# Probability blocks from SBUF to SBUF by sixteen small transfers a unit, in place of a way through DRAM

## The chip, the cores and the metric

The kernel runs on one core of one Trainium2 chip. The metric is the device time of one launch in microseconds (us); lower is better. A second clock is the profile: one execution recorded by the hardware profiler, whose span goes from the first to the last instruction. Engines are named PE (TensorE), PEld (its weight loads), DVE (VectorE), ACT (ScalarE), POOL (GpSimd) and SP (SyncE, which in this kernel does nothing but issue transfers).

## The reference

`x` has 8 batches of 256 tokens of 512 features, all in float32. It is normalised, goes through causal attention with 32 query heads and 8 key heads of 128 features, and the result is gated by the SiLU of a routed low-rank expert layer and added to `x`. The part that matters here is the middle of the attention:

```python
q = (xn @ wq.T) ; k = (xn @ wk.T) ; v = (xn @ wv.T)      # 32, 8 and 8 heads of 128
q, k = rope(q), rope(k)                                  # four query heads share a key head
scores = einsum('bhqd,bhkd->bhqk', q, k) / sqrt(128) * scale + causal
probs = softmax(scores)
attn = einsum('bhqk,bhkd->bhqd', probs, v)
out = x + (attn @ wo.T) * silu(ffn(xn))
```

## The kernel before

**Tiling.** The work goes in four rounds `tb` of two batches. In a round there are eight steps `g`, one for each key head, and in a step two *units*, one for each batch: 64 units in all. A unit is the attention of four query heads over 256 tokens. `softmax` (line 748) holds its first half and `values` (line 873) its second. PE also makes queries, keys and values by a Strassen-like scheme of seven products (`quad`, line 553), and the output projection by the same scheme (`out_project`, line 908).

**Softmax of a unit.** PE makes the scores with, in each of the 128 rows, one of 32 queries of one of four heads (row = 32 x head + query). DVE subtracts the maximum, ACT takes exponentials into the one tile `probs_sb` (`p` in the profile), DVE divides by the row totals. The values product needs the probabilities with the *keys* in the rows. DVE transposes 32x32 blocks, in two instructions, into the tile `blocks` (line 811), of which there is one for the whole kernel. That leaves each block inside its own group of 32 rows: group h of `blocks` holds, for head h, the four key groups j side by side. What is still missing is a move between groups: block (h, j) must go from rows 32h.. to rows 32j.., into the tile `pT`, of which there are three.

**The way through DRAM.** `spread` (line 822) writes `blocks` to a DRAM tile `there` in four transfers, one for each head, of 192 KB each. `gather` (line 832) reads it back into `pT` in one transfer of 768 KB. All five are issued on SP. SP waits for the second DVE transpose before the four, and for the landing of all four before the fifth.

**Values of a unit.** `values` makes two PE pieces, k = 0 for heads 0 and 1 and k = 1 for heads 2 and 3, of six matrix products each (`av`). Both wait for the unit's gather.

**The order of the work.** [...]That order comes from a planner (`Plan`, line 170) that simulates the kernel when it is built. Each job has an engine, an assumed time `takes`, and a `lag` after it until its result is there (a transfer's landing); `HOP`, 0.18 us, is added between jobs. PE's jobs are laid in a preferred sequence; every other job has a due time. A job can open a `hold` (take a buffer) and close it (give it back); `rooms` (line 298) has one room for `p`, one for `blocks` and three for `pT`. An engine takes the ready job with the earliest due time that has room. `softmax` adds `out_` (SP, 2.4 us, lag 3.4) and `in_` (SP, 0.35 us, lag 7.0); the hold on `blocks` ends with `out_`. The tile framework then puts in the semaphore waits. SP's transfers use eight semaphores in rotation, so the ninth transfer waits until the first has landed.

**Other work on SP.** Loads of `x`, of the gates and of the input for the last sum, the stores, and in three rounds the moves of the next round's normalised input (`norm`, lines 379 and 390): eight transfers of 128 KB to DRAM (`turned`) and eight back (`XB`). Weights are loaded by POOL's queue.

In the profile every instruction has line 118, that of a helper that issues them all, so the rows are told apart by tile names.

Of the kernel before, what the change touches and what calls it, by code (L numbers as in the profile page):

```python
# [37 lines left out]
F32 = mybir.dt.float32  # L38
# [6 lines left out]
P = 128  # L45
B, S, D = 8, 256, 512
H, KV, HD = 32, 8, 128
G = H // KV
# [7 lines left out]
NTB = B // NB  # L56
NT = TB // P
DC = D // P
BLK = 32
NI = S // BLK  # L60
NQ = P // BLK
# [108 lines left out]
class Plan:  # L170
# [10 lines left out]
    def add(self, engine, takes, what, after=(), opens=(), closes=(), near=None, lag=0.0):  # L181
        after = [a for a in after if a]
        job = Job(engine, takes, what, after, opens, closes, near, lag, len(self.jobs))
        for a in after:
            a.then.append(job)
        for hold in closes:
            hold.readers += 1
        self.jobs.append(job)
        return job
# [67 lines left out]
def layer(ctx: ExitStack, tc: tile.TileContext, x, wquad, woquad, raT, bT, table, out):  # L257
    nc = InOrder(tc)
# [4 lines left out]
    three = pool("three", 3)  # L263
# [28 lines left out]
    add = plan.add  # L292
    rooms = {}

    def hold(tag):
        return Hold(rooms[tag])
# [7 lines left out]
    keys, vals, queries, probs, attn, acc = {}, {}, {}, {}, {}, {}  # L304
# [443 lines left out]
    def softmax(tb, g, b):  # L748

        n = f"{tb}_{g}_{b}"  # L750
        box = {}
        p = probs_sb
# [12 lines left out]
        def scores(rows):  # L765
            kk = kbox["k"][:, g % G].rearrange("p i s -> p (i s)")
            sc = box["sc", rows] = ps_sc.tile(
                [P, width(rows)], F32, tag="sc", name=f"sc{n}_{rows[0]}"
            )
            for i, size, cols in spans(rows):  # L770
                first = P if i >= NQ else 0
                nc.tensor.matmul(
                    sc[:, cols], lhsT=qbox["q"][:, i].rearrange("p h s -> p (h s)"),
                    rhs=kk[:, first : first + size], start=True, stop=True,
                )
# [35 lines left out]
        def transpose(late):  # L811


            if not late:
                box["blocks"] = one.tile([P, NQ, 3 * P], F32, tag="blocks", name=f"blocks{n}")
            to, of = (
                (box["blocks"][:, :, 2 * P :], p[:, NQ:, NQ:]) if late
                else (box["blocks"][:, :, : 2 * P], p[:, :NQ])
            )
            nc.vector.transpose(to, of.rearrange("p j i c -> p j (i c)"))  # L820
# [11 lines left out]
        def gather():  # L832
# [3 lines left out]
                in_=box["there"].rearrange("j a h c -> (j a) (h c)"),  # L836
            )

        takes = lambda rows: sum(max(0.235, (i + 1) * 0.054) for i in rows)
        pieces, exps = [], []  # L840
        ph, bh, th = hold("p"), hold("blocks"), hold("pT")
        for rows in groups:
            sh, zh = hold("sc"), hold("z")
            sc = add(
                "pe", takes(rows), lambda r=rows: scores(r), after=[q_done, k_done], opens=[sh],
                closes=[qh, kh],
            )
# [7 lines left out]
                    opens=[ph] if rows == groups[0] else [], near=(sc, 2.5))  # L855
            )
            pieces.append(sc)
        sc = pieces[-1]
# [4 lines left out]
            near=(sc, 4.0),  # L863
        )
        t1 = add(
            "dve", 0.6, lambda: transpose(True), after=[t0], closes=[ph], near=(sc, 4.5)
        )
        out_ = add("sp", 2.4, spread, after=[t1], closes=[bh], near=(sc, 5.0), lag=3.4)
        in_ = add("sp", 0.35, gather, after=[out_], opens=[th], lag=7.0)
        probs[tb, g, b] = box, th, in_  # L870
        return pieces

    def values(tb, g, b):
        n = f"{tb}_{g}_{b}"
        pbox, ph, p_done = probs.pop((tb, g, b))
        vbox, vh, v_done = vals[tb, g // G, b]
        pieces = []


        def of(k):  # L880
            heads = slice(2 * k, 2 * k + 2)
            box = {}

            def work():
                v = vbox[b][:, :, bass.ts(g % G, HD)]
                pT = pbox["pT"][:, heads]
                av = box["av"] = ps_av.tile([P, 2, 2, P], F32, tag="av", name=f"av{n}_{k}")
                for t, block, keys_ in ((0, 0, 0), (1, 1, 0), (1, 2, 1)):
                    nc.tensor.matmul(
                        av[:, :, t, :], lhsT=v[:, keys_, :], rhs=pT[:, :, block, :],  # L890
                        start=block == 0, stop=block != 1, skip_group_check=True,
                    )

            def read():
                box["a"] = a_pool.tile([P, 2, S], F32, tag="a", name=f"a{n}_{k}")
                nc.scalar.copy(box["a"], box["av"].rearrange("p h t q -> p h (t q)"))

            h, ah = hold("av"), hold("a")
            av = add("pe", 1.3, work, after=[p_done] + v_done, opens=[h], closes=[ph, vh])
            a = add("act", 0.5, read, after=[av], opens=[ah], closes=[h], near=(av, 1.0))  # L900
            attn[tb, g, b, k] = box, ah, a
            pieces.append(av)

        for k in range(2):
            of(k)
        return pieces
# [468 lines left out]
    for n in range(len(steps) + 2):  # L1375
        last = n >= len(steps)
        tb, g = (NTB, 0) if last else steps[n]
        sa, sb = (ahead.pop(u, None) or part(softmax, u) for u in (NB * n, NB * n + 1))
        va, vb = (part(values, u - LAG_V) for u in (NB * n, NB * n + 1))
        ob = out_project(*steps[n - 1]) if 0 < n <= len(steps) else []  # L1380
# [17 lines left out]
        if n == len(steps) - 2:  # L1398

            ahead = {u: softmax(*units[u]) for u in (NB * n + 2, NB * n + 3)}  # L1400
            a1, b1 = ahead.values()
            fill = va[:1] + sa + va[1:]
            later = sb[:1] + oa[:1] + sb[1:] + oa[1:] + a1 + vb + ob[:2] + b1
        elif n == len(steps) - 1:
            fill, later = [], oa + va + vb + ob[:2]
        elif n == len(steps):
            fill, later = va + vb, oa + ob[:2]
# [37 lines left out]
```

## Time and profile before

| | |
|---|---|
| median of three runs | 1350.63 us (1345.75 to 1352.09) |
| profiled execution: time, span | 1350.19 us, 1348.4 us |
| mean granted TensorE clock | 0.998 |
| PE first matmul, last matmul ends | 6.6 us, 1342.2 us |
| transfers: bytes, share of the DMA engines' time | 282.10 MB; 35.9% POOL's queue, 31.8% SP's queue |
| SP issues through DRAM | 256 spreads of 192 KB, 64 gathers of 768 KB |

A row of the waits view reads: engine and what it was about to write, what ended its idle time, then total us, times, and the longest. A row of the timeline reads: start in us, length in us, engine, line, instruction, tiles written and read, shape, count, and in brackets the idle time just before. "SPq" is SP issuing a transfer: its length is the issue, not the transfer. In the view of a tile, "min/median/max" of an instruction are in ns.

### The profile page before, as it was taken

Reading aid. Unit: us, or ns where it says so; the run is one execution under the profiler, and the core shown is the slowest. Engines: PE = TensorE matmul, PEld = TensorE weight load, DVE = VectorE, ACT = ScalarE, POOL = GpSimd, SP = SyncE. Lnnn points to the kernel's source line nnn. Section 1 sums busy time; section 2 is a strip of 40 time slices with the busy share of each in tenths; the row PEclk is TensorE's granted clock in tenths of the full one; section 3 lists DMA queues with packets and bytes.
Section 4 is the critical chain, followed back from the end, with each engine's and each line's share of the span. In section 5 each row is a group of like instructions: output and inputs, shape, how many; then the busy total and the mean of one; then the engine's idle time right before and its main releaser. Section 6 shows DMA issues by size and latency. Waiting matters only on the chain.

```text
span 1348.4 us, 19893 instructions
## 1 busy us (share of the span) xinstructions
PE 1325.3 (98%) x6464; PEld 1165.7 (86%) x6464; DVE 1104.6 (82%) x2835; ACT 611.1 (45%) x1576; POOL 314.3 (23%) x579
## 2 busy tenths in 40 slices
PE   7999999999999999999999999999999999999998
PEld 6887888888889888888888988888888898888886
DVE  6899989998888768789697886969869787686997
ACT  3465444543534535354353443535444454434531
POOL 2322222222222122222222122222122211222010
PEclk9999999999999999999999999999999999999999
DMA  6577767686856666768676676676866676666584
GB/s 199 169 244 249 218 186 239 207 265 206 254 166 200 220 209 183 229 214 215 197 230 196 207 215 202 185 231 203 246 203 202 218 219 202 195 188 199 140 284 133
DMA packets 134182, 282.10 MB, mean 209 GB/s; under 512 B 40832, under 2 KB 80896, under 8 KB 134080
## 3 DMA queue, kind: packets, MB, share of 16 engines
q0 software_dynamic: 45760, 149.98, 35.9%
q1 hardware_dynamic: 88096, 130.19, 31.8%
q8 instruction: 52, 0.85, 0.2%
q10 hardware_dynamic: 224, 0.66, 0.2%
q14 instruction: 50, 0.41, 0.1%
HBM read 197.94 MB, written 82.84 MB: 208 GB/s over the span
## 4 chain that ended last, share of the span: by engine, by line
PE 75%; DVE 14%; DMA 6%; SPq 2%; issue 1%; ACT 1%; DVEq 0%; ACTq 0%
PE po L118 20%; PE paq L118 14%; PE av L118 9%; PE sc L118 7%; PE pdq L118 6%; DMA pT<-there 4%; PE pak L118 4%; PE pav L118 4%; PE peq L118 3%; DVE blocks L118 2%; PE pdk L118 2%; DVE acc L118 2%; SPq L118 2%; DVE qTq L118 2%; DVE p L118 2%; PE pdv L118 2%
## 5 line engine op out<-in xcount | busy, mean ns | idle before, releaser
L118 ACT ACTIVATE p<-z,least 128x256 f32<-128x256 f32 (+7 forms) x512 | 207.6, 407 | 203.0 <-DVE least L118 130.2
L118 PE MATMUL po<-wo,a 128*128 128x256 f32 x992 | 233.0, 379 | 0.0
L118 PEld LDWEIGHTS po<-wo,a 128*128 128x128 f32 x992 | 186.6, 190 | 22.9
L118 PE MATMUL av<-pT,v 128*128 128x256 f32 x768 | 186.3, 382 | 8.0 <-DMA pT<-there 8.0
L118 PE MATMUL paq<-XT,w 128*128 128x256 f32 x768 | 182.1, 380 | 0.3 <-ACT u3q L118 0.3
L118 DVE CUSTOM_DVE_ANT_0 z<-sc,tab 128x256 f32<-128x256 f32 (+7 forms) x512 | 134.4, 301 | 55.9 <-PE sc L118 52.8
L118 PE MATMUL po<-wo,s 128*128 128x256 f32 x744 | 177.6, 382 | 0.2 <-PE av L118 0.2
L118 PEld LDWEIGHTS av<-pT,v 128*128 128x128 f32 x768 | 145.6, 191 | 29.6 <-issue 5.6
L118 PEld LDWEIGHTS sc<-kk,qTq 128*128 128x128 f32 x1024 | 159.1, 191 | 12.8 <-DVE p L118 0.8
L118 PE MATMUL sc<-kk,qTq 128*128 128x256 f32 (+7 forms) x1024 | 168.1, 302 | 0.1
L118 PEld LDWEIGHTS paq<-XT,w 128*128 128x128 f32 x768 | 144.7, 190 | 20.2 <-ACT u2q L118 0.8
L118 POOL DMA_DIRECT2D w<-sums x144 | 79.2, 550 | 349.7 <-PE paq L118 143.9
L118 PEld LDWEIGHTS po<-wo,s 128*128 128x128 f32 x744 | 139.3, 190 | 23.4 <-issue 5.5
L118 ACT COPY a<-av 128x512 f32<-128x512 f32 x128 | 74.1, 580 | 180.5 <-PE av L118 180.2
L118 DVE TENSOR_TENSOR acc<-acc,po 128x512 f32<-128x512 f32 x189 | 127.9, 677 | 33.0 <-PE po L118 31.6
L118 ACT COPY swq<-cq 64x1024 f32<-64x1024 f32 x128 | 133.7, 1045 | 15.3 <-DVE cq L118 11.1
L118 POOL DMA_DIRECT2D w<-in_wquad_dram x148 | 80.9, 548 | 244.3 <-PE paq L118 85.2
L118 DVE STREAM_TRANSPOSE blocks<-p 128x1024 f32<-128x1024 f32 (+1 forms) x128 | 124.0, 970 | 0.2
L118 DVE TENSOR_SCALAR p<-p,total 128x256 f32<-128x256 f32 (+7 forms) x512 | 117.3, 295 | 2.3
L118 DVE TENSOR_TENSOR qTq<-cq,tab 128x1024 f32<-128x1024 f32 x64 | 78.0, 1219 | 25.3 <-ACT cq L118 25.1
L118 ACT ACTIVATION_READ_ACCUMULATOR p<-z,least 128x1 f32 x512 | 95.8, 187 | 0.0
L118 POOL DMA_DIRECT2D wo<-in_woquad_dram x104 | 56.9, 548 | 130.8 <-PE po L118 120.7
(135 smaller groups left out, 1855.0 us busy)
## 6 DMA issues: line engine op xcount, KB each, us to landing
there<-blocks SPq DMA_DIRECT2D x256, 192.0 KB, 3.9
pT<-there SPq DMA_DIRECT2D x64, 768.0 KB, 6.1
w<-in_wquad_dram POOLq DMA_DIRECT2D x148, 256.0 KB, 4.6
w<-sums POOLq DMA_DIRECT2D x144, 256.0 KB, 4.0
wo<-in_woquad_dram POOLq DMA_DIRECT2D x104, 256.0 KB, 5.0
wo<-osums POOLq DMA_DIRECT2D x96, 256.0 KB, 4.7
sums<-w POOLq DMA_DIRECT2D x48, 256.0 KB, 4.1
osums<-wo POOLq DMA_DIRECT2D x32, 256.0 KB, 5.0
```

The costliest lines, as they stand in the source:

```text
L118: ins = what(*args, **kwargs)
```

## The change

Units of the last round's last three steps (six units) keep the way through DRAM. For the other 58 units each of the sixteen blocks (head h, key group j), 32 rows of 1536 bytes, 48 KB, is moved by a transfer of its own from `blocks` straight into `pT`. They form two SP jobs of eight transfers: k = 0 moves heads 0 and 1, k = 1 heads 2 and 3. Each is planned at 4.5 us with a lag of 2.7. The second is planned after the first's landing, and the hold on `blocks` ends when both are through. The values piece k waits for job k alone, where before both pieces waited for the gather.

```diff
+        def straight(k):
+
+            if k == 0:
+                box["pT"] = three.tile([P, G, 3, P], F32, tag="pT", name=f"pT{n}")
+            for h in (2 * k, 2 * k + 1):
+                for j in range(NQ):
+                    nc.sync.dma_start(
+                        out=box["pT"][bass.ts(j, BLK), h].rearrange("p i c -> p (i c)"),
+                        in_=box["blocks"][bass.ts(h, BLK), j, :],
+                    )
...
-        out_ = add("sp", 2.4, spread, after=[t1], closes=[bh], near=(sc, 5.0), lag=3.4)
-        in_ = add("sp", 0.35, gather, after=[out_], opens=[th], lag=7.0)
-        probs[tb, g, b] = box, th, in_
+        if tb == NTB - 1 and g >= KV - 3:
+
+            out_ = add("sp", 2.4, spread, after=[t1], closes=[bh], near=(sc, 5.0), lag=3.4)
+            there = [add("sp", 0.35, gather, after=[out_], opens=[th], lag=7.0)] * 2
+        else:
+            there = []
+            for k in range(2):
+                there.append(
+                    add("sp", 4.5, lambda k=k: straight(k), after=[t1] + there,
+                        opens=[] if k else [th], closes=[bh], near=(sc, 5.0), lag=2.7)
+                )
+        probs[tb, g, b] = box, th, there
...
-            av = add("pe", 1.3, work, after=[p_done] + v_done, opens=[h], closes=[ph, vh])
+            av = add("pe", 1.3, work, after=[p_done[k]] + v_done, opens=[h], closes=[ph, vh])
```

## The prediction

> **What bounds the kernel.** I read the page's first rows, then PE's waits, then the timeline around those waits, then the views of the two tiles between which the change moves data. The engine row of the page, and all of PE's waits:
>
> ```profile
> PE 1325.3 (98%) x6464; PEld 1165.7 (86%) x6464; DVE 1104.6 (82%) x2835; ACT 611.1 (45%) x1576; POOL 314.3 (23%) x579
> ```
> ```profile
> PE av L118 <- DMA pT<-there: 8.0, 6, 3.0
> PE xp L118 <- DVE xn L118: 7.6, 2, 6.6
> PE pak L118 <- DMA w<-in_wquad_dram: 0.8, 1, 0.8
> PE paq L118 <- ACT u3q L118: 0.3, 1, 0.3
> PE po L118 <- PE av L118: 0.2, 1, 0.2
> ```
>
> PE is the bound. Its span less its busy time is 1348.4 - 1325.3 = 23.1 us, made of 6.6 us before the first matmul, 6.2 us after the last, and waits in between; at the start it waits for the normalised input (7.6, of which 6.6 is that first stretch). The only wait of the steady state is the first row: six values products that waited 8.0 us in all for the gather. So whatever the change does for transfers, PE can win about 8 us by it directly. The largest but one of these waits, in PE's timeline, and the stretches around it (columns of the second: PE, PEld, DVE, ACT, POOL, then granted clock, DMA share, GB/s):
>
> ```profile
> 639.62 3.62 PE L118 MATMUL po<-wo,a 128*128 128x256 f32 x16
> 645.53 2.54 PE L118 MATMUL av<-pT,v 128*128 128x256 f32 x6 [2.29 <-DMA pT<-there]
> 647.86 2.65 PE L118 MATMUL pak<-XT,w 128*128 128x256 f32 x8
> 650.34 1.89 PE L118 MATMUL pdk<-XT,w 128*128 128x256 f32 x8
> ```
> ```profile
> 645.50:649.50 4.00, 3.97 (x11) 3.21 (x12) 3.61 (x4) 0.58 (x1) 0.00 (x0) 0.57 0.26 54
> 649.50:660.00 10.50, 10.50 (x50) 9.26 (x49) 1.33 (x2) 3.57 (x6) 3.72 (x7) 1.00 0.52 156
> ```
>
> The six `av` products take 2.54 us instead of 1.46, and the clock granted is 0.57 for 4 us. So this wait cost its 2.29 us and another 4 x (1 - 0.57) = 1.7 us. The wait of 2.97 us at 114.5 was followed by a clock of 1.00 and cost nothing more.
>
> Now the tile `blocks`, read by the spreads, and the issues:
>
> ```profile
> L118 SPq DMA_DIRECT2D there<-blocks x256: 302/438/1523, 70.9 to 1313.9; - x128
> DMA to landing us min/median/max: 2.3/3.9/6.4
> ```
> ```profile
> there<-blocks SPq DMA_DIRECT2D x256, 192.0 KB, 3.9
> pT<-there SPq DMA_DIRECT2D x64, 768.0 KB, 6.1
> ```
>
> From the timeline of each unit I took the time from the end of its second transpose to the gather's landing: median 12.2 us, 9.2 to 17.1. The planner assumes 0.18 + 2.4 + 3.4 + 0.18 + 0.35 + 7.0 + 0.18 = 13.7. The changed units that made PE wait are all above it: 17.1 (third unit, 114.5), 14.6, 15.0, 16.6 (645.5) and 14.5.
>
> **The change, part by part.** *Removed*, 58 times: four issues (2.3 us of SP), SP's wait for their landing, a gather. *Added*, 58 times: sixteen issues of 48 KB.
>
> Issue: inside a spread the next issue starts 476 ns after the last (median of 191), the eight loads at the kernel's start 474 ns apart. A straight transfer has 32 rows where a spread has 128 pieces, so it should cost no more; bounds are 345 ns (the shortest distance between spreads) and 978 ns (`XB<-turned`, with 1024 pieces). I take 476. Landing: 2.3 us is the least for a spread, of four times the bytes; 3.9 is the median with three others in flight. I take 2.3 to 4. Eight semaphores mean that the ninth issue waits for the first landing; that is 8 x 0.476 = 3.8 us later, so in quiet it waits for nothing, and at a landing of 6.4 each transfer costs 6.4 / 8 = 0.8 us.
>
> So k = 0 is there 7 x 0.476 + 2.3 = 5.6 us after the transpose (7.3 at a landing of 4), k = 1 15 x 0.476 + 2.3 = 9.4 (11.1). Against 12.2 median and 17.1 worst, first halves come 5 to 10 us earlier and second halves 1 to 6. The planner assumes 0.18 + 4.5 + 2.7 + 0.18 = 7.6 for k = 0 and 15.0 for k = 1, more than I expect of the chip: its PE order leaves room where the old one had too little.
>
> Here a rule speaks against the change. The Trainium skill, DMA: Bandwidth & Descriptors, "Rules for kernel authors", says to coalesce many small transfers, since below 64 KB one pays mostly overhead; its "Anatomy of one DMA" puts some 2.0 us on each, whatever its size. The row of a spread's landing (2.3 us least) shows the same 2 us, but four are in flight together, 476 ns apart: overhead is paid as delay, not as throughput. If sixteen paid it in turn, a unit would take 16 x 2.1 = 34 us, more than the 1348 / 64 = 21 us that a unit has, and the kernel would be far slower. By the rows it is 9.4. I go by the rows; SP's 58 x 16 x 0.476 = 442 us of issue fit its 1348 (it issued for 250 before, of which about 150 go).
>
> Traffic: a changed unit moves 768 KB once, not twice, and nothing to or from DRAM. SP's queue has 31.8% of the DMA engines' time; that falls and helps POOL's weight loads, which cost PE 0.8 us in all. I count nothing for it.
>
> Waits on PE: a values piece reads eight transfers with eight semaphores instead of one. PE's sequencer spends 51 ns on a waiting instruction, which covers two. Four for each of 116 pieces is between 0 and 116 x 4 x 51 ns = 24 us. Near row: ahead of the products at 628.5 stand three such instructions, for four SP and one POOL transfer, and the products kept their distance of 216 ns; they were queued ahead of need. I take 0. Behind a waiting piece everything on PE is queued.
>
> Waits on DVE: the first transpose of the next unit now waits for sixteen transfers. Two more waiting instructions, 58 times, at 50 to 100 ns are 6 to 12 us of DVE, which idles 244 us; nothing on the path. But the tile is held longer, 9.4 to 11.1 us after the transpose where it was 5 to 7. From the timeline, the next unit's first transpose came 8.3 us or more after (mostly near 20); of the first 58 units, 14 came under 15.0, eight under 9.9. If the order of DVE stayed, the eight would wait 5.5 us in all. It doesn't stay: the planner now holds `blocks` for 15.0 us and puts other DVE work before those transposes, so on the chip the tile should be free when DVE comes to it. Late are then the transposes themselves, by up to 6.7 us, with queued behind them on ACT the next unit's exponentials (one `p`). Eight of these fourteen had 10 to 18 us between their gather's landing and their use, which covers it; three had 3 to 5 and three under 1.3, two of them in the start. There the cover is thin: units follow each other by 12 to 15 us against a planned least of 17, and by the fourth they are about 10 us behind. There PE has other products within the planner's 30 us of looking ahead. I charge 1.5 us, between 0 and 10.
>
> SP: behind the sixteen issues (7.6 us) stand the moves of the next round's input, three times; `XB` of the second batch landed at 640.8 with its products at 648.1 and two sums between. Four more issues ahead of it are 1.9 us, all sixteen 7.6: between 0 and 3 x 3 us. I take 0, for it is planned too.
>
> Sum against the profiled 1350.19: the pT waits 8.0, less 0.25 of one in the last six units that stay as they are, gives 7.75; with the clock after the 645.5 wait, 1.7, it is 9.45; less 1.5 for the start: -7.95, so 1342.2. The median of the runs stands 0.44 above the profiled execution, so 1342.7, said as 1342.5. The least would be 1350.2 - 9.5 = 1340.7.
>
> **Rivals.** *The waits change place* (28%): the longer planned hold of `blocks` turns the start and the round changes into new waits of 5 to 10 us. For it: one `blocks`, one `p`, 14 near units. Against: the slack above. Time: 1346 to 1352. The case that the change doesn't do what it says also ends here: if PE's piece k = 0 waited for all sixteen, both halves would be there at 9.4 to 11.1, still under the plan's figure for k = 1 but over the 7.6 for k = 0, and some of the 8 us would stay.
>
> *Slower: the rate of small transfers* (20%): if one takes not 0.48 but 1.0 us, as `XB<-turned` does, the hold is 15 x 1.0 + 2.3 = 17.3 us, 2.3 over the plan's 15.0, and DVE, in order, stands at the transposes while PE's banks stay full behind it. Fourteen near units x 2.3 = 32 us of DVE, with k = 1 pieces late by the same; a third to all of it reaches PE, which gives 1342.5 + 11 to 32 = 1354 to 1375, most likely 1366. It decides from (15.0 - 2.3) / 15 = 0.85 us a transfer.
>
> **How the numbers follow.** The forecast has 52%, the two rivals 28% and 20%. A measurement can tell about 0.5% from no change: under 1343.9 counts as faster, over 1357.4 as slower. Of the forecast's 52, 44 lie under 1343.9; with 1 of the first rival that makes 45% faster; 18 of the second and 1 of the first make 19% slower; 36% between. The range goes from 1337 (the least, less the spread of runs, about 0.3%) to 1358, which takes in the forecast, the first rival and the foot of the second; nearly all of what is left out is the slow rival.
>
> **What would show it.** Right: no row of PE waiting for `pT` above 1 us in all, straight issues 0.4 to 0.5 us apart, landings of 2 to 4 us, first transposes not waiting on transfers, clock 1.00 at 645. Wrong: distances above 0.85 us, DVE waiting for `pT<-blocks`, or new PE rows before 130 us or at the round changes.

## The result and the profile after

The changed kernel takes 1351.03 us (median of 20 runs, 1347.35 to 1356.44) against 1347.48 (1344.88 to 1352.83, 20 runs) for the kernel before: a ratio of 1.0025, 95% interval 1.0014 to 1.0035. That is a small loss, under the 0.5% that I had called measurable. I had forecast 1342.5. The time is in the range, but the direction is wrong.

The page's engine row and all of PE's waits above 0.2 us after the change:

```profile
PE 1325.7 (98%) x6464; PEld 1167.0 (86%) x6464; DVE 1103.8 (82%) x2835; ACT 607.7 (45%) x1576; POOL 314.2 (23%) x579
```
```profile
PE xp L118 <- DVE xn L118: 6.6, 1, 6.6
PE av L118 <- DMA pT<-blocks: 5.9, 3, 3.5
PE pak L118 <- DMA XB<-turned: 4.8, 1, 4.8
PE sc L118 <- DVE least L118: 1.0, 1, 1.0
PE pak L118 <- ACT XB L118: 0.7, 1, 0.7
```

The row that the change was to remove, `av` waiting for `pT<-there`, is gone. In its place stand `av` waiting for the straight transfers and, new, `pak` (keys) waiting for the next round's input. PE's timeline shows where both are (in brackets the idle time before a row):

```profile
94.48 1.89 PE L118 MATMUL paq<-XB,w 128*128 128x256 f32 x8
99.90 1.75 PE L118 MATMUL av<-pT,v 128*128 128x256 f32 x6 [3.53 <-DMA pT<-blocks]
101.45 1.33 PE L118 MATMUL sc<-kk,qTq 128*128 128x96 f32 x6
102.59 2.91 PE L118 MATMUL peq<-XB,w 128*128 128x256 f32 x8
```
```profile
298.50 1.57 PE L118 MATMUL sc<-kk,qTq 128*128 128x192 f32 x12
304.91 3.75 PE L118 MATMUL pak<-XB,w 128*128 128x256 f32 x8 [4.84 <-DMA XB<-turned]
...
318.59 1.53 PE L118 MATMUL av<-pT,v 128*128 128x256 f32 x6 [1.45 <-DMA pT<-blocks]
```

Both long waits were followed by a slow clock, seen in the length of the next rows (2.91 us for eight products instead of 1.89) and in the clock column, after POOL, of these two stretches:

```profile
99.90:104.00 4.10, 4.10 (x15) 3.62 (x16) 0.83 (x1) 1.63 (x2) 1.02 (x2) 0.64 0.90 260
304.90:309.50 4.60, 4.59 (x11) 3.72 (x12) 1.84 (x2) 0.80 (x2) 0.54 (x1) 0.52 0.57 102
```

So 4.1 x 0.36 = 1.5 us and 4.6 x 0.48 = 2.2 us come on top. After 320 us PE has no new wait worth a row; the three rounds behind are better than before. What SP did ahead of the wait at 304.9:

```profile
284.52 5.59 SPq L118 DMA_DIRECT2D pT<-blocks  x8
290.21 3.93 SPq L118 DMA_DIRECT2D turned<-x  x4
294.26 6.24 SPq L118 DMA_DIRECT2D XB<-turned  x4
300.54 5.24 SPq L118 DMA_DIRECT2D pT<-blocks  x8
```

The first eight straight transfers of a unit go first, then the second batch's move to DRAM, which takes 3.93 us to issue, and only then the first batch's way back (`XB`), which PE needs. The last product on the old input ended at about 290.5; `XB` was issued from 294.3, some 3.7 us later, and landed at 304.7. In the kernel before that product ended at 288.4, both moves to DRAM were already issued, `XB` followed at 288.5 and had landed by 298.3:

```profile
278.00 5.80 SPq L118 DMA_DIRECT2D turned<-x  x8
283.90 0.80 SPq L118 DMA_DIRECT2D pT<-there  x1
288.46 6.19 SPq L118 DMA_DIRECT2D XB<-turned  x4
```

### The profile page after: what moved, and what is told of

The parts are those of the page before. It is cut to its first block, busy times and chain, and to the rows that moved or that the text cites. A ratio compares the mean times of both kernels' runs of the same rounds, so it can differ in the third digit from the quotient of the medians.

```text
span 1351.4 us, 21044 instructions
## 1 busy us (share of the span) xinstructions
PE 1325.7 (98%) x6464; PEld 1167.0 (86%) x6464; DVE 1103.8 (82%) x2835; ACT 607.7 (45%) x1576; POOL 314.2 (23%) x579
## 2 busy tenths in 40 slices
DMA packets 136973, 236.60 MB, mean 175 GB/s; under 512 B 51040, under 2 KB 91104, under 8 KB 136864
## 4 chain that ended last, share of the span: by engine, by line
PE 84%; SPq 2%; DVE 1%; issue 1%; DMA 1%; POOL 0%; DVEq 0%; POOLq 0%
PE po L118 26%; PE paq L118 14%; PE av L118 11%; PE sc L118 9%; PE pdq L118 7%; PE peq L118 4%; PE pav L118 4%; PE pak L118 3%; PE pdv L118 2%; PE pdk L118 2%; SPq L118 2%; PE dle L118 1%; PE pev L118 1%; PE lme L118 1%; DVE acc L118 1%
## 5 line engine op out<-in xcount | busy, mean ns | idle before, releaser
L118 PEld LDWEIGHTS sc<-kk,qTq 128*128 128x128 f32 x1024 | 159.9, 191 | 13.7 <-DVE least L118 1.4
```

The source lines that it names most:

```text
L118: ins = what(*args, **kwargs)
```

## The experiments

Times stand beside runs of the kernel before on the same chip; each ratio is to those.

**Where the loss sits.** First round through DRAM again:

```diff
-        if tb == NTB - 1 and g >= KV - 3:
+        if tb == 0 or tb == NTB - 1 and g >= KV - 3:
```

> The sixteen units of the first round go through DRAM again, as the last six do; the 42 units between stay straight. Theory S (sixteen issues a unit keep SP busy for about 10 us and, while POOL still stores sums in the first round, land late and push back the moves of the next round's input): the new waits at 85, 100, 151, 305 and 319 us go, the gain of rounds 2 to 4 (the wait at 645.5 with its clock, 4.0 us, and 0.4 at 976) stays: 3 to 5 us under the kernel before. Theory H (the longer planned hold of the one tile of blocks makes a worse order): the same in the first round, but some cost stays in rounds 2 to 4: within 1 us of the kernel before. Theory W (more semaphore waits on PE and DVE for each values piece, everywhere): 2 to 3 us over the kernel before.

Measured 1343.27 us, ratio 0.9968 (0.9957 to 0.9978), 4.7 us under the kernel before. The straight transfers of rounds 2 to 4 do bring what was forecast, and the loss sits in the first round and its end. Theory W falls with this, and so does theory H's cost in the later rounds. Two parts of that region, each put back alone (`tb == 0 and g < 2`, and `tb == 0 and g in (5, 6)`):

> The changed kernel with its first four units through DRAM as well, the other 54 of the 58 straight. Theory place (two separate places cost: the start, and the change from the first round to the second, where the next input's moves queue on SP behind straight transfers): the waits at 85, 100 and 151 us go, that at 305 us with its slower clock stays: 4 to 8 us under the changed kernel. Theory lottery: the order of everything is dealt anew, and the wait at the round change moves as well.

> The changed kernel with units 10 to 13 (counted from 0), those around the change from the first to the second round, through DRAM as well. Theory place: the waits at 305 and 319 us with the slower clock after them, some 8 us, go; those of the start stay: 6 to 9 us under the changed kernel. Theory lottery: other waits of like size in their place, within 3 us of the changed kernel.

Measured 1345.18 (0.9983, 0.9972 to 0.9995) and 1345.33 (0.9983, 0.9969 to 0.9998). Each takes back 1.0025 - 0.9983 = 0.42%, about 6 us. By size each could be a place of its own, but together they make 0.84%, where the whole first round gave 0.57%. And the waits did not stay where the theory put them: with the start through DRAM the wait for `XB` at the round change fell to 0.7 us as well, and with the round change through DRAM it was still 2.3. The planner deals the later order anew with every edit, so places are not independent.

**Is it the number of issues?** The same planner's figures, but two transfers of 64 rows by 3072 bytes in a job for eight of 32 by 1536; the blocks come to wrong rows:

```diff
-            for h in (2 * k, 2 * k + 1):
-                for j in range(NQ):
...
+            for a in range(2):
+                nc.sync.dma_start(
+                    out=box["pT"][bass.ts(a, 2 * BLK), 2 * k : 2 * k + 2].rearrange("p h i c -> p (h i c)"),
+                    in_=box["blocks"][bass.ts(k, 2 * BLK), 2 * a : 2 * a + 2].rearrange("p j c -> p (j c)"),
+                )
```

> The changed kernel with the same planner's figures, but each of its two jobs a unit issues two transfers of 64 rows by 3072 bytes instead of eight of 32 by 1536: the same bytes from SBUF to SBUF with a quarter of the issues. The blocks then come to wrong rows, so the values are those of mixed-up probabilities. Theory S: SP is free after some 2.5 us, data land 4 to 6 us after the transpose, the five new waits go: 8 to 12 us under the changed kernel, so 4 to 8 under the kernel before. Theory H: the planner's hold is the same, so the time is that of the changed kernel within 2 us.

Measured 1341.38, ratio 0.9959 (0.9947 to 0.9972). This is what theory S said, and theory H falls: with the same figures and the same planned hold the time is 0.66% under the changed kernel's. First halves now landed 4.7 us after the transpose (median of the 58 units), second halves 8.2, where the plan has 7.6 and 15.0; five first halves and four second ones were later than the plan. PE still waited 2.0 and 1.3 us at the round change. So the order that the change's figures make is not bad in itself: it is bad because the chip doesn't keep to them.

**Is it the order, or the figures?** All units through DRAM, but with the blocks given back 15 us after the transpose in the plan, by an empty job after the spreads (the lines not shown here take the branch through DRAM always, and let the spreads give the blocks back in the last six units alone):

```diff
...
+                add("dma", 0.0, lambda: None, after=[out_], closes=[bh], near=(sc, 8.0), lag=8.6)
```

> All units through DRAM as in the kernel before, but the planner gives the tile of blocks back 15 us after the transpose, as the change makes it do, for all but the last six units. No transfer changes, only the order of the work. Theory H: 3 to 8 us over the kernel before, with new waits in the start. Theory S: within 1.5 us of the kernel before.

Measured 1351.84, ratio 1.0041 (1.0025 to 1.0056): the size that theory H said. Yet its waits are for the gather (8.8 us in seven), whose latency of up to 18.0 us the plan still took for 13.7. And the next runs speak against the hold alone. The changed kernel with what the chip took:

```diff
-                    add("sp", 4.5, lambda k=k: straight(k), after=[t1] + there,
-                        opens=[] if k else [th], closes=[bh], near=(sc, 5.0), lag=2.7)
+                    add("sp", 5.1, lambda k=k: straight(k), after=[t1],
+                        opens=[] if k else [th], closes=[bh], near=(sc, 5.0 + 0.1 * k), lag=3.6)
```

> The changed kernel with the planner told what the chip took: eight issues 5.1 us (633 ns apart) instead of 4.5, landing 3.6 us after them instead of 2.7, and the second eight free to follow the first at once instead of after their landing. Theory S: most waits of the first round stay, since SP is as busy: within 2 us of the changed kernel. Theory P (only the planner's figures were wrong, so PE was sent to wait): the waits at 100 and 305 us go: 6 to 10 us under the changed kernel.

Measured 1340.58, ratio 0.9957 (0.9944 to 0.997): theory P. Theory S had the waits stay, for SP is as busy; they went. The transfers are the same as the changed kernel's; only their place among the other work differs. All of PE's waits above 0.4 us:

```profile
PE xp L118 <- DVE xn L118: 6.6, 1, 6.6
PE av L118 <- DMA pT<-blocks: 1.5, 3, 0.7
PE pak L118 <- ACT XB L118: 0.7, 1, 0.7
PE av L118 <- DMA XB<-turned: 0.5, 1, 0.5
PE po L118 <- DVE s L118: 0.5, 1, 0.5
```

and SP at the same round change:

```profile
271.45 4.48 SPq L118 DMA_DIRECT2D turned<-x  x8
277.10 10.74 SPq L118 DMA_DIRECT2D pT<-blocks  x16
287.95 5.03 SPq L118 DMA_DIRECT2D XB<-turned  x4
295.46 10.04 SPq L118 DMA_DIRECT2D pT<-blocks  x16
```

Both moves to DRAM are out of the way before the straight transfers, `XB` is issued at 288.0 and landed at 296.6, and PE uses it at 297.6 without a wait. DVE waits longer for straight transfers than in the changed kernel (17.7 us in four waits against 13.0 in seven), and that doesn't reach PE.

With a longer lag than in the version just shown, and about the planned hold of the change (by the sum of the prediction 15.2 us, where the change has 15.0):

```diff
-                        opens=[] if k else [th], closes=[bh], near=(sc, 5.0 + 0.1 * k), lag=3.6)
+                        opens=[] if k else [th], closes=[bh], near=(sc, 5.0 + 0.1 * k), lag=4.6)
```

> The informed plan with a lag of 4.6 instead of 3.6. Theory figures or chain: within 2 us of the informed plan, since both cover what the chip takes. Theory lottery (any new figure deals a new order of all work, and times scatter by 4 us whatever it says): more than 3 us away from it.

Measured 1343.42, ratio 0.9954 (0.9938 to 0.9971). A planned hold of 15 us is not what costs.

**Which half of that edit?** The figures and the chain (second job after the first's landing) apart. Where the chain is left out, here and above, the second job's due time is 0.1 us later:

```diff
-                    add("sp", 4.5, lambda k=k: straight(k), after=[t1] + there,
-                        opens=[] if k else [th], closes=[bh], near=(sc, 5.0), lag=2.7)
+                    add("sp", 4.5, lambda k=k: straight(k), after=[t1],
+                        opens=[] if k else [th], closes=[bh], near=(sc, 5.0 + 0.1 * k), lag=2.7)
```

> The changed kernel with one thing less: the second eight transfers are planned to follow the first at once, not after their landing; figures as in the change (4.5 and 2.7). Theory chain (planning the second job after the first's landing leaves a gap on SP into which the next round's moves are put, and holds the blocks for 15 us): the gain of the informed plan comes back, 6 to 10 us under the changed kernel. Theory figures (4.5 and 2.7 are too short, so PE is sent to values products before the data): 0 to 4 us under the changed kernel, with waits for straight transfers left.

```diff
-                    add("sp", 4.5, lambda k=k: straight(k), after=[t1] + there,
+                    add("sp", 5.1, lambda k=k: straight(k), after=[t1] + there,
...
-                        opens=[] if k else [th], closes=[bh], near=(sc, 5.0), lag=2.7)
+                        opens=[] if k else [th], closes=[bh], near=(sc, 5.0), lag=3.6)
```

> The changed kernel with the measured figures (5.1 and 3.6), but the second eight still planned after the first's landing, so the planned hold of the blocks is 17.8 us. Theory figures: 6 to 10 us under the changed kernel. Theory chain: the changed kernel's time or up to 5 us more, since the hold grows.

Neither theory held. Without the chain: 1357.85, ratio 1.0062 (1.0045 to 1.008). With the figures and the chain: 1380.12, ratio 1.0225 (1.0205 to 1.0245). Each half alone makes it worse, both together make it 0.7% better than the change. The reading that fits: without the chain the plan expects second halves at 12.1 us, where the chip took 14.0 (median; 11.5 to 17.1) and 52 of 58 were late, and PE has waits before `av` of 12.8 us in all, the largest of them:

```profile
PE av L118 <- DMA gates<-gatese: 4.4, 2, 2.6
PE av L118 <- DMA pT<-blocks: 4.2, 3, 2.6
PE av L118 <- issue: 1.8, 3, 1.2
PE av L118 <- DMA turned<-x: 1.4, 1, 1.4
```

(the first and the last row name transfers that `av` does not read, but that use the same eight semaphores of SP).

With the chain and the true figures only nine first halves and six second ones were later than planned, so late transfers are not the cost. The plan holds the blocks for 17.9 us after the transpose, 20 us for a whole unit, against the 21 that a unit has, and the units fall behind from the start: the last changed unit's transpose came at 1268 us, at 1233 in the changed kernel and 1223 in the informed one. PE was idle for 36.5 us between products, where it was for 19.4 in the changed kernel, and busy 9.8 us longer, at a mean clock of 0.992. This loss is in the plan itself. The planner's own reckoning, which each kernel file makes when it is built, ends PE's work at 1357.7 us here, at 1329.0 for the change (28.7 us apart; by the ratios the chip took some 27 us longer), and between 1328.3 and 1330.1 for all the other versions. With two rooms for `blocks` in that reckoning, or with the blocks given back after the first job, it ends at 1328.3 here too; this was reckoned and not run. So the long hold costs once it reaches 17.9 us, and everywhere else the versions differ by what the chip does not keep of an equally short plan. In the change the chain's wrong delay happened to cover the second halves' wrong figure, and nothing covered the first halves'.

**Would the old way have done as well?** The kernel before, with its own figures made true:

```diff
-        out_ = add("sp", 2.4, spread, after=[t1], closes=[bh], near=(sc, 5.0), lag=3.4)
-        in_ = add("sp", 0.35, gather, after=[out_], opens=[th], lag=7.0)
+        out_ = add("sp", 2.4, spread, after=[t1], closes=[bh], near=(sc, 5.0), lag=4.4)
+        in_ = add("sp", 0.35, gather, after=[out_], opens=[th], lag=8.5)
```

> The kernel before, all units through DRAM, with the planner told more of what its trace shows: landing of the spreads 4.4 us after their issue instead of 3.4, of the gather 8.5 instead of 7.0, so 16.2 us from the transpose to the data instead of 13.7. If the planner's figures alone set these waits: the 8 us of waits for the gather go, 5 to 7 us under the kernel before, as fast as the informed straight version. If the shorter way is needed: within 2 us of the kernel before.

Measured 1341.41, ratio 0.9936 (0.9919 to 0.9954). All of its PE waits but one of 0.2:

```profile
PE xp L118 <- DVE xn L118: 7.1, 2, 6.7
PE pak L118 <- DMA XB<-turned: 2.6, 1, 2.6
PE pak L118 <- ACT XB L118: 0.7, 1, 0.7
```

No transfer was changed, and not one wait for the gather is left. With 9.5 for the gather's lag:

> The kernel before with the spreads' landing planned at 4.4 us and the gather's at 9.5 (17.2 us from the transpose to the data, its measured maximum being 17.1). Theory figures: again no wait for the gather, within 2 us of the version with 8.5. Theory lottery: more than 3 us away from it.

Measured 1342.35, ratio 0.995 (0.9934 to 0.9967): the same within the intervals, which speaks against a lucky deal. Both findings together (first round through DRAM with 4.4 and 8.5, rounds 2 to 4 straight with 5.1 and 3.6):

> Both findings together: first round and last six units through DRAM with the figures 4.4 and 8.5, the 42 units between straight with 5.1 and 3.6 and no chain. Theory figures: no waits for probabilities at all, the least PE time of all versions, 7 to 9 us under the kernel before. Theory lottery: anywhere from 3 to 10 under it.

Measured 1341.92, ratio 0.9955 (0.9941 to 0.9968): no better than either. Its one long wait is for `XB` (2.2 us), and the 7 to 9 us expected were 6. Five versions whose figures were raised to what the chip took, none of them with the chain, are 0.4 to 0.6% under the kernel before, and can't be told apart; the least edit of them is two numbers in the old kernel.

## Why the prediction was wrong

**What bounds the kernel: right.** PE, with 8 us to win at the values products and 1.7 at the clock. All five waits for the gather are gone after the change, and the informed versions took 0.4 to 0.6% off, where my floor of 1340.7 is 0.7%.

**The step that failed: "more than I expect of the chip: its PE order leaves room where the old one had too little".** It rested on two mis-sized terms. The view of `blocks` after the change (its last line also covers the 24 spreads that stay):

```profile
L118 SPq DMA_DIRECT2D pT<-blocks x928: 507/589/1787, 68.6 to 1245.3; - x186
...
DMA to landing us min/median/max: 1.8/3.5/7.5
```

I took 476 ns from issue to issue, from transfers with DRAM at one end. From SBUF to SBUF it was 633, since the issue itself takes 589; 345 to 978 were my bounds. I took 2.3 to 4 us to landing: the median, 3.5, is inside, the tail (7.5) is not. So first halves were there after 8.1 us in the median (6.3 to 11.4), not 5.6 to 7.3, and 37 of 58 came after the plan's 7.6. Second halves took 14.0 (11.5 to 22.6), not 9.4 to 11.1; 17 came after the plan's 15.0. Theory and price of the slow rival were on the right term, but it set the turn at 0.85 us a transfer, by the hold of the blocks. The turn came earlier and elsewhere: at the first halves (3.53 + 1.45 of the 6.1 us that values products waited).

**The start: I charged 1.5 us.** It cost 0.94 + 3.53 + 0.98 of waits and 1.5 of clock, 7.0. Unit 1's first half, for which the 3.53 were, took 11.4 us where the plan had 7.6.

**SP at the round change: "I take 0, for it is planned too".** It cost 4.84 + 1.45 and 2.2 of clock, 8.5, just under the upper end that I had put there (9). The order that the planner had fixed put what PE needs behind transfers that took longer than planned. Being planned was no cover.

The sum then reads -9.45 + 7.0 + 8.5 = +6.1. The spans differ by 1351.4 - 1348.4 = 3.0. Of the other 3.1, 1.5 are waits that the sum leaves out: `xp` 1.0, a weight 0.8, `paq` 0.3 and the last gather 0.25 shorter, `pak` for ACT 0.7 and one issue 0.2 longer. The remaining 1.6 I can't place: by the clock PE's busy time should have risen by 1.5 + 2.2 - 1.7 = 2.0 us, and it rose by 0.4 (1325.3 to 1325.7). So the terms for the waits close, and those for the clock are not confirmed in sum.

**DVE at the transposes: wrong, and of no weight.** I had the tile free when DVE comes to it; DVE waited 13.0 us in seven for `pT<-blocks`. The informed version waited longer and was faster, so this is not what cost.

**The waits on PE: right at 0.** PE's waiting instructions went from 512 to 955. In front of the matrix products the excess over their usual distance is 0 in the median after one such instruction, and after two.

**The small-transfer rule: right to set aside as a rate, but not free.** Sixteen transfers did overlap: a unit's took 14.0 us to land, not 34. The cost was in SP's issuing: 654 us in all, not the 540 that my numbers make; the same bytes in a quarter of the issues landed in 8.2. The section "Anatomy of one DMA" of the Trainium skill's DMA: Bandwidth & Descriptors, from which I took 2.0 us, speaks of transfers that GpSimd issues. SP's landed after 1.8 us at the least from SBUF to SBUF, and after 2.3 from SBUF to DRAM.

**Traffic: right to count nothing.** The bytes fell from 282.10 to 236.60 MB and gave no time.

**What stays open.** The loss with the long hold in the DRAM way (1.0041) I can't fully take apart. Its plan ends no later than the others (1328.3), so it is not the planned hold as such; 23 of its 64 gathers were there after the plan's 13.7 us, where 15 were in the kernel before. Why places in the first round are not independent is argued from the planner, not shown step by step. A second tile for the blocks was not tried on the chip.

## What to carry to other kernels

Where a planner fixes the order of all engines, a changed transfer is two changes: what the chip does, and what the planner believes. Compare each assumed latency with the landing times of the trace, tail included, before blaming the transfer, and look at where the plan itself ends: it moved in one of the fourteen kernels here, and in the others the loss was what the chip did not keep. Here two numbers in the planner were worth as much as the new way at its best. Bound the first piece that someone waits for, not only the last, and treat "it is planned" as a claim to be checked against durations.

## What the runs showed of the hardware

Issues on SP stood 633 ns apart for transfers from SBUF to SBUF, whether of 48 KB in 32 rows or (638 ns) of 192 KB in 64, and 476 ns where one end was DRAM with 192 KB in 128 pieces. Size and rows made no difference between the first two. What makes the step to 476 isn't shown: `XB`, which comes from DRAM in 1024 pieces, stood 978 apart.

The slow clock came after PE waits of 2.29, 3.53 and 4.84 us, and did not after one of 2.97: the length of a wait alone doesn't tell. The traces of all the runs together say the same. After the first 20 us the granted clock stood at 0.5, for 3.41 us or two or three times as long, after all five waits of 3.4 us or more, after none under 1.8, and after about half of the 21 between.
